# Selective-scan and attention network on one core: the first delta on VectorE, operations with a lower bound on their place, and a new set of places

## Chip, cores and metric

The kernel runs on one core of one Trainium2 chip. The metric is the device time of one execution in microseconds, from three timed executions. The same program was also run once under the hardware profiler; that execution's own time and its span (first to last instruction) stand beside the three below.

A core has TensorE (PE, with its weight loads PEld), VectorE (DVE), ScalarE (ACT), GpSimd (POOL) and SyncE (SP). Each engine takes its instructions in the order of the program. In this kernel all DMA transfers are issued from SP, in the order of its queue.

## The reference, cut to what matters

Eight images of 384 channels and 32 x 32 positions pass two layers. The first is a selective scan in both directions with a gated local convolution; the second is causal attention with six heads and a feed-forward network.

```python
def mamba(x, ...):                      # once forwards, once on the reversed sequence; L = 1024
    u, z = split(x @ in_proj_w.T)
    u = silu(causal_conv4(u) + conv1d_b)
    dt, Bm, Cm = split(u @ x_proj_w.T)                    # 24, 16, 16 columns
    delta = softplus(dt @ dt_proj_w.T + dt_proj_b)
    h = exp(delta * A) * h + (delta * u) * Bm             # over the 1024 positions, 16 states
    y = (sum over states of h * Cm + u * D) * silu(z)
    return y @ out_proj_w.T

x1 = x + res_scale * (scale_mod * (fwd + bwd) + sigmoid(conv3x3(xn) + dw_b) * xn)
t = x1 + attention(layernorm(x1))
out = t + (gelu(layernorm(t) @ w_fc.T) @ w_proj.T)        # w_fc and w_proj are Kronecker products
```

## The kernel before

The kernel does not issue its instructions as it goes. Each piece of work is an `op(engine, cost, fn, reads, writes, at=...)`, which is only recorded; `Plan.run` (line 170) then orders all of them and the instructions are emitted in that order. What the plan decides is therefore the order on each engine's queue and the assignment of buffers, nothing else: on the chip no instruction waits for a time, only for its data, its buffers and the instructions in front of it.

`Plan.run` is a list scheduler. It keeps a time for each engine, and at each step takes the operation that can start first. Among operations of an engine that can start within 0.05 us of each other, the one with the smallest `at` (its place, in us) goes first. So a place is a rank: an operation with a late place is taken early if its engine has nothing else to do. A few rules modify this. ACT prefers the table that it has loaded by `STAY` us of rank (line 110). A DMA that was not given a place by hand waits until the modelled backlog of transfers is under 50 us. Buffers of a kind are handed out by place: 26 general tiles `t`, 12 `dA`, 3 PSUM banks `b`, 1 PSUM bank `y`, 4 PSUM banks `psm`.

Most places come from `Window` (line 446): the operations recorded inside one share the stretch from `t0` to `t1` in proportion to their costs. DMAs get their place earlier by `MOVE`, and ACT or DVE operations that touch a `psm` bank earlier by `EVICT`. The constants of lines 436 to 443 are these windows. Those in capital letters with a 0 or 1 at the end are in us; the others are in units of `PERIOD`, counted from `HEAD` plus the image's number times `PERIOD` (line 1397).

The work of one image:

- `project(b)` loads the image (`xt`) and half of the input weights (`win`), forms the norm (`sq` on ACT, `pss` on PE), writes `xp`, multiplies (`pi` on PE) and writes the rows to DRAM (`urd`).
- `gates(b)` multiplies with the other half of the weights and writes `uzd` and `xpd` to DRAM.
- `prepare(b)` reads shifted rows (`ct`), convolves them (`pc` on PE), applies SiLU (`u`) and forms `xd` (`px` on PE).
- `deltas(b)` calls `delta(b, d, c, ...)` for three blocks of 128 channels and two directions. `delta` computes softplus on ACT (line 891) and six elementwise operations of 128x1024 on POOL (lines 898, 899, 900, 902 and twice 913). Their results, `de` and the three bf16 parts of `du`, go to DRAM (`ded`, `dusd`).
- `scans(b)` runs 96 groups. Each loads `dA` from `ded` and, for every four, `du` from `dusd`; ACT takes the exponential (line 994), PE spreads `du` over the states (the `b` matmul of line 1009), DVE multiplies and scans two halves (lines 1005 and 1013), POOL multiplies by C (line 1016), and PE sums (`y`).
- `local`, `finish`, `layernorm`, `attention`, `mix`, `forward` do the rest for the image while later images are scanned.

The places of a scan group are given by hand from its step's time: loads at `-LOAD`, exponentials at `-DECAY`, POOL products at `-PRODUCTS`, sums at `-SUMS`; with a negative constant the place is later.

Before the first scan stand `setup_early`, `project(0)`, `prepare(0)`, the first `deltas(0)`, and `setup_zeros` (line 572), which writes zeros to the last quarter of each `dusd`. Set up for later use are `setup_late` (line 583: residual scales, local convolution weights `tapw`/`wlm`, `D2`) and `setup_layer1` (line 612: the attention weights copied to `wqkv` in DRAM, `bvc`, `w_fc1`, `w_p1`, `kr2`). The first reader of `bvc` is line 1282 of the attention.

Of the kernel before, what the change touches and what calls it, by code (L numbers as in the profile page):

```python
# [19 lines left out]
L = H * W  # L20
# [45 lines left out]
class Val:  # L66


    __slots__ = ("kind", "shape", "dtype", "name", "t", "slot", "writes", "reads", "left", "end", "first")
# [4 lines left out]


class Op:
    __slots__ = ("engine", "cost", "fn", "vals", "allocs", "at", "waits", "users", "ready", "table", "done", "nbytes", "index", "after", "placed", "urgent")


def act(n):  # L80
# [7 lines left out]
def pool(n):  # L88
    return 0.1 + n * 0.0022
# [15 lines left out]
class Plan:  # L105
# [1 line left out]
    DRAIN = 0.19  # L107
    SLACK = 0.1
    SWITCH = 1.3
    STAY = 50.0  # L110
    BACKLOG = 50.0
    LANDING = 1.0
    DMA_LATENCY, DMA_RATE = 2.5, 262e3
# [5 lines left out]
    def op(self, engine, cost, fn, reads=(), writes=(), at=None, table=None, nbytes=0, holds=()):  # L119


        o = Op()
        o.engine, o.cost, o.fn, o.table, o.nbytes = engine, cost, fn, table, nbytes
        o.at = self.at if at is None else at
        o.placed = o.urgent = at is not None
        o.vals, o.allocs, o.users, o.ready, o.done = [], [], [], 0.0, None
        deps = set()

# [3 lines left out]
        for v in reads:  # L132
            v, part = v if isinstance(v, tuple) else (v, None)
# [3 lines left out]
        for v in writes:  # L137
            v, part = v if isinstance(v, tuple) else (v, None)
# [31 lines left out]
    def run(self):  # L170
# [3 lines left out]
        ready = {e: [] for e in engines}  # L174
        dma = 0.0
        table = None
# [26 lines left out]
                release(owner[id(v)], t)  # L203

        for o in self.ops:
            if o.waits == 0:
                ready[o.engine].append(o)
        for kind in queue:
# [17 lines left out]
        while len(order) < total:  # L226
# [27 lines left out]
            start, e, o = best  # L254
# [33 lines left out]
def conv_attn_hybrid_kernel(  # L288
# [41 lines left out]
    def mm(out_, lhsT, rhs, first=True, last=True):  # L330
        return nc.tensor.matmul(out_, lhsT=lhsT, rhs=rhs, start=first, stop=last)  # L331
# [101 lines left out]

    EVICT, MOVE, SUMS, PRODUCTS, DECAY, LOAD, PARTS = 111.21, 8.82, 26.97, -2.67, -328.02, -584.01, -478.49

    PROJECT, GATES, CONV, DELTA = (-1.521, -1.371), (-1.067, -1.026), (-0.976, -0.866), (-0.889, -0.365)
    LOCAL, OUTPUT, NORM, ATTEND = (0.661, 0.853), (1.005, 1.032), (1.082, 1.173), (1.202, 1.761)
    MIX, FORWARD = (1.787, 1.854), (1.855, 2.07)  # L440

    PROJECT0, EARLY, CONV0, DELTA0 = (-400.622, -296.945), (-523.036, 67.185), (-160.273, 70.933), (131.8, 263.184)
    GATES0, ZEROS, LATE, PROJECT1, GATES1 = (177.592, 252.86), (56.018, 117.713), (263.977, 276.95), (-19.453, 206.415), (352.446, 448.404)
    CONV1, DELTA1, LAYER1 = (250.186, 263.964), (271.922, 425.403), (675.476, 1110.704)

    class Window:


        def __init__(self, t0, t1, start=0.0):
            self.t0, self.t1 = start + t0, start + t1  # L450

        def __enter__(self):
            self.first = len(plan.ops)
# [1 line left out]
        def __exit__(self, *_):  # L455
            ops = [o for o in plan.ops[self.first :] if not o.placed]
            total, done = sum(o.cost for o in ops), 0.0
            for o in ops:
                early = MOVE if o.engine == "SP" else 0.0
                if o.engine in ("DVE", "ACT") and any(v.kind == "psm" for v in o.vals):  # L460
                    early = EVICT
                o.at = self.t0 + (self.t1 - self.t0) * done / total - early
                done += o.cost
                o.placed = True


    def array(shape, name, dtype=F32):
# [400 lines left out]
    def delta(b, d, c, du, xd):  # L868
# [26 lines left out]
            nc.scalar.activation(w.t, w.t, AF.Identity, bias=minus)  # L895

        op("ACT", 4 * act(L) + 0.2, logs, [], [e, ln, w], table=EXP)
        op("POOL", pool(L), lambda: nc.gpsimd.tensor_sub(w.t, e.t, w.t), [e], [w])
        op("POOL", pool(L), lambda: nc.gpsimd.tensor_add(de.t, de.t, ln.t), [ln], [de])
        op("POOL", pool(L), lambda: nc.gpsimd.tensor_add(de.t, de.t, w.t), [w], [de])  # L900
        dma(lambda: ded[d][s].t[chans(c)], lambda: de.t, [de], [(ded[d][s], c)], P * L * 4)
        op("POOL", pool(L), lambda: nc.gpsimd.tensor_mul(du.t, de.t, du.t), [de], [du])
        for k in range(3):
            part = Val("t2", [P, L], f"part_{n}_{k}", BF16)
            op("ACT", act(L), lambda part=part: nc.scalar.copy(part.t, du.t), [du], [part])  # L905
            for hf in range(NH):
                dma(
                    lambda k=k, hf=hf: dusd[d][s].t[c * RG : (c + 1) * RG, hf, k],
                    lambda part=part, hf=hf: part.t[:, half(hf)], [part], [(dusd[d][s], (c, k, hf))], P * HALF * 2,
                )  # L910
            if k < 2:
                op(
                    "POOL", pool(L), lambda part=part: nc.gpsimd.tensor_sub(du.t, du.t, part.t), [part], [du]  # L913
                )

    def scans(b, t0, period):
# [63 lines left out]
    def group(b, a, d, j, r, at, du3, bc):  # L980
# [18 lines left out]
        halves = [(hf, Val("b", [P, HALF], f"b_{n}_{hf}")) for hf in (range(NH - 1, -1, -1) if d else range(NH))]  # L999
        for hf, v in halves:  # L1000
            rr = slice((r * NH + hf) * KI, (r * NH + hf + 1) * KI)
            op("PE", 0.24, lambda v=v, rr=rr: mm(v.t, dup[rr, :], du3.t[rr, j]), [du3], [v], at=-1000.0 + at * 1e-3)
        for i, (hf, v) in enumerate(halves):
            op(
                "DVE", dve(HALF), lambda v=v, hf=hf: nc.vector.tensor_mul(v.t, v.t, bc.t[:, 0, half(hf)]), [(bc, 0)], [v],  # L1005
# [388 lines left out]

    PERIOD, HEAD = 393.0, 65.75

    def stretch(span, b):
        return Window(span[0] * PERIOD, span[1] * PERIOD, HEAD + b * PERIOD)  # L1400
# [8 lines left out]
        deltas(0, *made)  # L1409
    with Window(*GATES0):  # L1410
        gates(0)
    with Window(*ZEROS):
        setup_zeros()
    with Window(*LATE):
        setup_late()
    with Window(*PROJECT1):
        project(1)
    with Window(*GATES1):
        gates(1)
    with Window(*LAYER1):  # L1420
        setup_layer1()
    for b in range(B):
        scans(b, HEAD + b * PERIOD, PERIOD)
# [96 lines left out]
```

## Time and profile before

| | us |
|---|---|
| three timed executions | 4003.02 (median), 3989.68, 4006.04 |
| the profiled execution | 4019.04 |
| its span | 4017.1 |
| first scan instruction starts | 153.2 |
| last scan instructions (L1013) end about | 3747 |
| ACT table loads (L1456), 226 of 1283 ns | 290.0 |
| dA loads, 768 of 512 KB; wait of ACT L994 for them | 234.0 |

The profile's groups are named by line, engine, operation and tile. The helper `dma` gives all transfers line 414 and the helper `mm` most matmuls line 331, so these are told apart by their tiles. "Idle before" is the time that an engine waited ahead of an instruction, with what ended the wait. The start of a transfer in the order of time is the start of its issue on SP, not its landing.

### The profile page before, as it was taken

The page shows a single profiled execution, that of the slowest core. Times are in us where ns is not written, and L with a number is a line of the kernel's source. Part 1 is how long each engine was busy: PE and PEld are TensorE (multiplying, and loading weights), DVE is VectorE, ACT ScalarE, POOL GpSimd, SP SyncE. Part 2 cuts the span into 40 slices and gives each one's busy share as a digit, 9 for nine tenths or more (in the row PEclk, how much of TensorE's full clock was granted, in tenths as well). Part 3 has the DMA queues.
Part 4 walks back from the last instruction along what each step waited for, and adds up shares of the span by engine and source line. Part 5 has one row for each costly group of instructions (what it writes and reads, how often), then busy time and mean ns, then how long its engine had stood idle before and what let it go on. Part 6 is the DMA issues. An engine that isn't in the chain of part 4 may idle for free.

```text
span 4017.1 us, 54053 instructions
## 1 busy us (share of the span) xinstructions
PE 3709.8 (92%) x17970; PEld 1404.8 (35%) x17970; DVE 3332.5 (83%) x4403; ACT 2825.4 (70%) x4468; POOL 2997.6 (75%) x2370
## 2 busy tenths in 40 slices
PE   7577879899999999999999999999999999999998
PEld 2111112443234432444224432444324432443363
DVE  1498979978988989889988999889998899999522
ACT  4756647776788857888678867888678867676364
POOL 1988877997579965899569975899669975776231
PEclk9677678899998999999999999989999999999998
DMA  7989997679976898769976799669986698578100
GB/s 249 270 243 262 255 258 218 178 225 239 270 213 179 236 238 259 205 187 251 269 232 199 226 253 285 190 185 255 260 242 194 181 255 240 147 192 218 49 20 25
DMA packets 301998, 858.92 MB, mean 214 GB/s; under 512 B 38312, under 2 KB 91576, under 8 KB 301720
## 3 DMA queue, kind: packets, MB, share of 16 engines
q1 hardware_dynamic: 301720, 855.47, 76.4%
q8 instruction: 143, 2.34, 0.3%
q14 instruction: 135, 1.11, 0.1%
HBM read 696.44 MB, written 160.68 MB: 213 GB/s over the span
## 4 chain that ended last, share of the span: by engine, by line
PE 53%; DVE 14%; DMA 10%; POOL 8%; issue 4%; ACT 2%; SPq 0%; POOLq 0%; DVEq 0%; ACTq 0%
DVE dA L1013 7%; PE b L331 7%; PE pc L331 6%; PE y L331 5%; PE pi L331 4%; DMA dA<-ded 4%; POOL dA L1016 4%; DVE b L1005 3%; PE t L1250 3%; PE s L331 3%; PE pk L331 3%; PE pvv L331 3%; PE pq L331 2%; DVE mx L1186 2%; POOL p L1240 2%
## 5 line engine op out<-in xcount | busy, mean ns | idle before, releaser
L1016 POOL TENSOR_TENSOR dA<-dA,bc 128x1024 f32<-128x1024 f32 x768 | 1806.1, 2363 | 605.0 <-DVE dA L1013 506.4
L1013 DVE TENSOR_TENSOR_SCAN dA<-dA,b 128x512 f32<-128x512 f32 x1536 | 1854.3, 1234 | 92.7 <-ACT dA L994 90.3
L1005 DVE TENSOR_TENSOR b<-b,bc 128x512 f32<-128x512 f32 x1536 | 996.9, 681 | 173.2 <-PE b L331 161.4
L994 ACT ACTIVATE dA<-dA,nA 128x1024 f32<-128x1024 f32 x768 | 863.4, 1145 | 272.3 <-DMA dA<-ded 234.0
L331 PE MATMUL b<-du,dup 32*128 32x512 bf16 x1536 | 609.4, 408 | 181.0 <-DVE dA L1013 158.8
L331 PE MATMUL y<-dA,sel 128*32 128x512 f32 x3072 | 489.2, 663 | 11.2 <-POOL dA L1016 8.3
L331 PEld LDWEIGHTS <-dup 32*128 32x128 bf16 x1536 | 132.9, 92 | 935.4 <-issue 903.0
L1186 DVE TENSOR_REDUCE mx<-s 128x1 f32<-128x512 f32 (+3 forms) x576 | 288.7, 547 | 186.1 <-PE s L331 182.3
L1240 POOL TENSOR_SCALAR p<-p,den 128x512 f32<-128x512 f32 (+3 forms) x576 | 327.1, 586 | 86.0 <-DVE den L1232 79.3
L1193 ACT ACTIVATE p<-s,mx 128x512 f32<-128x512 f32 (+3 forms) x576 | 329.4, 578 | 75.0 <-DVE mx L1186 74.1
L1257 ACT COPY pT<-t 128x512 f32<-128x512 f32 (+2 forms) x480 | 245.9, 546 | 129.2 <-PE t L1250 123.1
L331 PE MATMUL pi<-xp,win 128*128 128x512 f32 x576 | 312.4, 650 | 10.4 <-DVE xp L696 4.5
L1250 PE MATMUL t<-ident,p 128*128 128x128 f32 x1728 | 281.6, 298 | 29.7 <-POOL p L1240 14.0
L1456 ACT ACT_TABLE_LOAD x226 | 290.0, 1283 | 4.0
L331 PE MATMUL s<-k,q 64*128 64x512 f32 (+3 forms) x1152 | 283.7, 544 | 9.2 <-ACT p L1193 8.6
L1250 PEld LDWEIGHTS t<-ident,p 128*128 128x128 f32 x1728 | 200.1, 149 | 164.8 <-issue 74.0
L331 PE MATMUL pc<-pT,v 128*64 128x128 f32 x3456 | 251.0, 289 | 5.3 <-ACT pT L1257 4.9
L331 PEld LDWEIGHTS pc<-pT,v 128*64 128x64 f32 x3456 | 193.9, 142 | 100.5 <-ACT pT L1257 31.2
L913 POOL TENSOR_TENSOR u<-u,part 128x1024 f32<-128x1024 f32 x96 | 204.9, 2134 | 10.5 <-ACT part L905 9.9
L905 ACT CAST part<-u 128x1024 bf16<-128x1024 f32 x144 | 150.5, 1045 | 64.8 <-DMA dusd<-part 49.9
L1365 ACT ACTIVATE g<-ph 128x512 f32<-128x512 f32 x192 | 104.1, 595 | 118.4 <-PE ph L331 117.4
L331 PEld LDWEIGHTS y<-dA,sel 128*32 128x32 f32 x3072 | 75.4, 112 | 286.2 <-issue 152.6
(184 smaller groups left out, 4776.1 us busy)
## 6 DMA issues: line engine op xcount, KB each, us to landing
dA<-ded SPq DMA_DIRECT2D x768, 512.0 KB
ct<-urd SPq DMA_DIRECT2D x96, 513.5 KB
du<-dusd SPq DMA_DIRECT2D x96, 512.0 KB
xs<-xpd SPq DMA_DIRECT2D x96, 432.8 KB
dusd<-part SPq DMA_DIRECT2D x288, 128.0 KB
ded<-de SPq DMA_DIRECT2D x48, 512.0 KB
uz<-uzd SPq DMA_DIRECT2D x48, 512.0 KB
bc<-bcd SPq DMA_DIRECT2D x32, 512.0 KB
```

Of the source, the lines that this page charges most:

```text
L331: return nc.tensor.matmul(out_, lhsT=lhsT, rhs=rhs, start=first, stop=last)
L913: "POOL", pool(L), lambda part=part: nc.gpsimd.tensor_sub(du.t, du.t, part.t), [part], [du]
L994: "ACT", act(L) + 0.1, lambda: nc.scalar.activation(dA.t, dA.t, AF.Exp, scale=nA.t[:, g : g + 1]),
L1005: "DVE", dve(HALF), lambda v=v, hf=hf: nc.vector.tensor_mul(v.t, v.t, bc.t[:, 0, half(hf)]), [(bc, 0)], [v],
L1013: nc.vector.tensor_tensor_scan(t, t, v.t[:, rev], h, ALU.mult, ALU.add)
L1016: op("POOL", pool(L), lambda: nc.gpsimd.tensor_mul(dA.t, dA.t, bc.t[:, 1]), [(bc, 1)], [dA], at=at - PRODUCTS)
L1186: lambda sc=sc, g=g, w=k1 - k0, hh=hh: nc.vector.tensor_reduce(mx.t[:, g, hh : hh + 1], sc[hh].t[:, 0:w], AX.X, ALU.max, negate=True), [sc ...
L1193: nc.scalar.activation(ps[g].t[:, hh, 0 : k1 - k0], sc[hh].t[:, 0 : k1 - k0], AF.Exp, bias=mx.t[:, g, hh : hh + 1], accum_out=den.t[:, g, ...
L1240: nc.gpsimd.tensor_scalar(t, t, den.t[:, g, hh : hh + 1], 1.0, ALU.mult, ALU.mult)
L1250: nc.tensor.transpose(t.t[:, o + j * P : o + (j + 1) * P], ps[g].t[:, hh, j * P : (j + 1) * P], ident)
L1257: nc.scalar.copy(pT[g].t[:, hs[0] : hs[-1] + 1, 0:w], t.t[:, 0 : len(hs) * w].rearrange("p (h w) -> p h w", w=w))
L1456: nc.scalar.preload_act_table_set(table)
```

## The change

Four things are changed together.

1. The six elementwise operations of `delta` go to DVE, with a cost of 1.2 in the plan, for the first image's first block in the first direction. All other deltas keep POOL.
2. A window can be `held`: its operations are not ready in the plan before their place. `ZEROS`, `LATE`, `PROJECT1` and `LAYER1` are held.
3. All constants of places are new, with `PERIOD`, `HEAD`, and `STAY` 25 in place of 50.
4. The plan's cost of a `b` matmul is 0.325 in place of 0.24.

No instruction besides these six changes engine, and no data is computed in another way.

```diff
-    __slots__ = ("engine", ..., "placed", "urgent")
+    __slots__ = ("engine", ..., "placed", "urgent", "held")
...
-    STAY = 50.0
+    STAY = 25.0
...
         o.placed = o.urgent = at is not None
+        o.held = False
...
         for o in self.ops:
+            if o.held:
+                o.ready = o.at
             if o.waits == 0:
                 ready[o.engine].append(o)
...
-    EVICT, MOVE, SUMS, PRODUCTS, DECAY, LOAD, PARTS = 111.21, 8.82, 26.97, -2.67, -328.02, -584.01, -478.49
+    EVICT, MOVE, SUMS, PRODUCTS, DECAY, LOAD, PARTS = 82.85, 10.31, 27.98, -31.81, -95.38, -1000.42, -591.88

-    PROJECT, GATES, CONV, DELTA = (-1.521, -1.371), (-1.067, -1.026), (-0.976, -0.866), (-0.889, -0.365)
-    LOCAL, OUTPUT, NORM, ATTEND = (0.661, 0.853), (1.005, 1.032), (1.082, 1.173), (1.202, 1.761)
-    MIX, FORWARD = (1.787, 1.854), (1.855, 2.07)
+    PROJECT, GATES, CONV, DELTA = (-1.524, -1.369), (-1.117, -1.031), (-0.978, -0.848), (-0.925, -0.363)
+    LOCAL, OUTPUT, NORM, ATTEND = (0.668, 0.848), (1.0, 1.02), (1.149, 1.17), (1.202, 1.761)
+    MIX, FORWARD = (1.784, 1.828), (1.855, 2.047)

-    PROJECT0, EARLY, CONV0, DELTA0 = (-400.622, -296.945), (-523.036, 67.185), (-160.273, 70.933), (131.8, 263.184)
-    GATES0, ZEROS, LATE, PROJECT1, GATES1 = (177.592, 252.86), (56.018, 117.713), (263.977, 276.95), (-19.453, 206.415), (352.446, 448.404)
-    CONV1, DELTA1, LAYER1 = (250.186, 263.964), (271.922, 425.403), (675.476, 1110.704)
+    PROJECT0, EARLY, CONV0, DELTA0 = (-245.3, -129.175), (-714.373, 90.417), (-128.151, 81.389), (29.762, 164.363)
+    GATES0, ZEROS, LATE, PROJECT1, GATES1 = (225.887, 251.93), (29.21, 60.597), (208.002, 221.031), (-257.494, 100.613), (376.438, 377.438)
+    CONV1, DELTA1, LAYER1 = (127.612, 279.646), (321.852, 516.462), (580.149, 926.317)
...
-                o.placed = True
+                o.placed, o.held = True, self.held
...
-        op("POOL", pool(L), lambda: nc.gpsimd.tensor_sub(w.t, e.t, w.t), [e], [w])
-        op("POOL", pool(L), lambda: nc.gpsimd.tensor_add(de.t, de.t, ln.t), [ln], [de])
-        op("POOL", pool(L), lambda: nc.gpsimd.tensor_add(de.t, de.t, w.t), [w], [de])
+        first = b == 0 and d == 0 and c == 0
+        name, cost, engine = ("DVE", 1.2, nc.vector) if first else ("POOL", pool(L), nc.gpsimd)
+        op(name, cost, lambda: engine.tensor_sub(w.t, e.t, w.t), [e], [w])
+        op(name, cost, lambda: engine.tensor_add(de.t, de.t, ln.t), [ln], [de])
+        op(name, cost, lambda: engine.tensor_add(de.t, de.t, w.t), [w], [de])
         dma(lambda: ded[d][s].t[chans(c)], lambda: de.t, [de], [(ded[d][s], c)], P * L * 4)
-        op("POOL", pool(L), lambda: nc.gpsimd.tensor_mul(du.t, de.t, du.t), [de], [du])
+        op(name, cost, lambda: engine.tensor_mul(du.t, de.t, du.t), [de], [du])
...
-                    "POOL", pool(L), lambda part=part: nc.gpsimd.tensor_sub(du.t, du.t, part.t), [part], [du]
+                    name, cost, lambda part=part: engine.tensor_sub(du.t, du.t, part.t), [part], [du]
...
-            op("PE", 0.24, lambda v=v, rr=rr: mm(v.t, dup[rr, :], du3.t[rr, j]), [du3], [v], at=-1000.0 + at * 1e-3)
+            op("PE", 0.325, lambda v=v, rr=rr: mm(v.t, dup[rr, :], du3.t[rr, j]), [du3], [v], at=-1000.0 + at * 1e-3)
...
-    PERIOD, HEAD = 393.0, 65.75
+    PERIOD, HEAD = 405.15, 84.77
...
-    with Window(*ZEROS):
+    with Window(*ZEROS, held=True):
         setup_zeros()
-    with Window(*LATE):
+    with Window(*LATE, held=True):
         setup_late()
-    with Window(*PROJECT1):
+    with Window(*PROJECT1, held=True):
         project(1)
...
-    with Window(*LAYER1):
+    with Window(*LAYER1, held=True):
         setup_layer1()
```

## The prediction, made before the changed kernel was run

> **What bounds the kernel now.** I read the page's engine totals first, then its chain of waits, then busy time by stage, then the order of time around the start. All fences are of the kernel before.
>
> ```profile
> PE 3709.8 (92%) x17970; PEld 1404.8 (35%) x17970; DVE 3332.5 (83%) x4403; ACT 2825.4 (70%) x4468; POOL 2997.6 (75%) x2370
> ...
> PE 53%; DVE 14%; DMA 10%; POOL 8%; issue 4%; ACT 2%; SPq 0%; POOLq 0%; DVEq 0%; ACTq 0%
> ```
>
> No engine is full, but TensorE is nearest and has half of the chain. Cut into stages by the scans (first at 153, 192 per image, last at 3747 us), busy time reads:
>
> ```profile
> 0.00:152.00 152.00, 104.24 (x293) 40.47 (x294) 18.37 (x74) 85.84 (x110) 58.41 (x63) 0.89 0.81 247
> 152.00:547.00 395.00, 299.16 (x974) 61.51 (x973) 351.76 (x407) 240.95 (x256) 353.40 (x173) 0.69 0.92 259
> 547.00:995.00 448.00, 401.97 (x2035) 154.87 (x2035) 392.18 (x514) 304.10 (x495) 372.13 (x291) 0.89 0.80 220
> ...
> 1905.00:2360.00 455.00, 440.66 (x2242) 169.95 (x2240) 414.14 (x542) 354.13 (x561) 372.30 (x291) 0.99 0.83 234
> ...
> 3750.00:4017.00 267.00, 248.66 (x1319) 126.48 (x1318) 70.29 (x141) 129.06 (x327) 54.84 (x146) 0.96 0.09 33
> ```
>
> After the stretch come PE, PEld, DVE, ACT, POOL busy, the granted clock, the DMA share and GB/s. Four regimes: a start of 152 us in which nothing is scanned; the first image, with DMA at 0.92 and VectorE at 351.8 of 395; the steady images, with TensorE at 440.7 of 455, so 14 us idle; and a tail of 267 us on TensorE, with 18 us idle. What shortens the start moves all that follows. In the steady part an order can win back at most TensorE's gaps, unless it also lets the first scans do more.
>
> The start's last links, in the order of time on POOL, SyncE's queue and VectorE:
>
> ```profile
> 102.24 2.35 POOL L898 TENSOR_TENSOR w<-e,w 128x1024 f32<-128x1024 f32 x1 [19.22 <-ACT w L895]
> 104.54 2.37 POOL L899 TENSOR_TENSOR de<-de,ln 128x1024 f32<-128x1024 f32 x1
> 106.98 2.35 POOL L900 TENSOR_TENSOR de<-de,w 128x1024 f32<-128x1024 f32 x1
> 109.41 2.35 POOL L902 TENSOR_TENSOR u<-de,u 128x1024 f32<-128x1024 f32 x1
> 111.72 2.36 POOL L898 TENSOR_TENSOR w<-e,w 128x1024 f32<-128x1024 f32 x1
> 114.03 2.14 POOL L913 TENSOR_TENSOR u<-u,part 128x1024 f32<-128x1024 f32 x1
> 116.11 2.37 POOL L899 TENSOR_TENSOR de<-de,ln 128x1024 f32<-128x1024 f32 x1
> 118.43 2.15 POOL L913 TENSOR_TENSOR u<-u,part 128x1024 f32<-128x1024 f32 x1
> ```
>
> ```profile
> 126.85 2.48 SPq L414 DMA_DIRECT2D dusd<-part  x2
> 129.86 3.95 SPq L414 DMA_DIRECT2D uzd<-us  x2
> 133.90 2.49 SPq L414 DMA_DIRECT2D dusd<-part  x2
> 136.49 1.99 SPq L414 DMA_DIRECT2D ded<-de  x1
> 138.53 2.73 SPq L414 DMA_DIRECT2D dA<-ded  x2
> 141.30 0.58 SPq L414 DMA_DIRECT2D du<-dusd  x1
> ```
>
> ```profile
> 151.99 1.30 DVE L1005 TENSOR_TENSOR b<-b,bc 128x512 f32<-128x512 f32 x2 [77.58 <-PE b L331]
> ```
>
> The six POOL operations of the first delta run from 102.2 to 120.6 us with two of the second delta between them. The third part is cast at 122.5 to 123.6 on ACT, written at 126.9, and the du load that needs it is issued at 141.3, behind writes of the second delta (133.9, 136.5). It lands 10 us later. VectorE had idled for 77.6 us.
>
> **What the Trainium skill says.** "VectorE: DVE Perf Modes", section The TRN2 errata, gives an fp32 tensor_tensor of N elements (N+151)/0.96 ns; my estimate from that page for N=1024 is 1.22 us. The trace has the 128x512 product with a PSUM operand at 681 ns and two of them in 1.30 us, which agrees in size; 128x1024 with both operands in SBUF is not in it. "SBUF — State Buffer", section Who interferes with whom, says that a VectorE instruction with two SBUF inputs contends with a POOL instruction that reads SBUF. No row separates this out. "ScalarE: Activation LUTs", What ACT_TABLE_LOAD costs, gives 1283 ns and a drain; the page's row has 226 loads of 1283 ns, and L1456 shows no such drain as idle time (4.0 us in all). "Perfetto Trace Analysis", Identifying the Most-Contended Engine, warns that matmul busy time is no measure of roofline. So I use TensorE's gaps only as an upper bound on what an order can return.
>
> **Part by part.** The sum is against the profiled execution's 4019.0 us (span 4017.1, 2 us around it). This lies 16 us above the median of 4003.0 and above the highest of the three, so I carry the difference over to the median.
>
> 1. First delta on VectorE. Removed from POOL: 4 x 2.35 + 2 x 2.14 = 13.7 us. Added on VectorE: 6 x 1.2 = 7.2 us, in the 77.6 us in which it idles, so the engine time is free. On the path 6.5 us go from the operations and up to 4.7 from the second delta's two in between. ACT can give some back: its logs of the second delta (105.3 to 109.8) may stand before the first cast. From 102.2, 7.2 of VectorE and three casts of 1.05 put the third part near 113, with hand-overs 114, against 123.6. The du load waits behind the second delta's writes, but POOL reaches these earlier too, free of 13.7 us. I take -9; bounds -12 and -5 (if every VectorE operation waits for a POOL one through the shared port). If VectorE's idleness were gone it would cost 7.2 us of its own queue.
>
> 2. Weights of layer 1 (LAYER1, held). Their 16 DMA issues run at 20.2 to 36.1 us, 12.2 us on SyncE, and move 2.3 MB. Behind them in the queue stands urd<-ut, issued at 36.8 though its first rows were evicted at 30.4; the ct loads, which wait for urd, begin at 44.2. Held, the weights go to places 570 to 800, where the 650:700 slice of the trace has a DMA share of 0.67. In their stead come eight zero writes (ZEROS, place 24 to 47), 10.6 us of issue at 71.9 now. So one block of the queue replaces another, partly later: -4, bounds -9 and +3. The eight POOL selects on kr (4.0 us) go into a stage where POOL has 76 us free. bvc's place is 707 and the first reader of bvc runs at 717.3; if attention comes 16 us earlier, finished contexts hold the four PSUM banks for up to about 10 us. I cost it at 0, bound +10.
>
> 3. The second image's projection (PROJECT1). Its new window opens at -257, ahead of PROJECT0's -245: its three image loads, at -268 to -257, are placed before the first image's at -256 to -252. Three such loads land 1.3 us apart now (sq starts at 13.6, 14.9, 16.2), so the first projection slips by +4. In return its pss matmuls, which stand between the last conv matmuls from 64.3 to 70.9 us, should be over by then: -6.6 if so, since u is finished at 75.4 only after the last conv. I take -4 for this return, bounds -6.6 and 0; the part's net is 0. Holding itself binds only for the last 28% of the window, which is past time 0.
>
> 4. LATE, held at about 200 to 221. The nine tapw loads that block SyncE for 12.3 us at 271 move some 70 us earlier, and the scans go from 14 to 7 in that slice now; the block stays. The two D loads, issued at 18.8 us now, are needed by the first y at 219.5. With 12 dA buffers, about 46 us of scans at 3.83 each, a lateness of some us is absorbed. 0, bounds -5 and +8.
>
> Parts 1 to 4: -9 - 4 + 0 + 0 = -13, bounds -29 and +20.
>
> 5. New places, STAY 25, and the 0.325 for the b matmul. They add and remove no instruction except table loads; they reorder all five queues. Moved most is LOAD, by which dA loads go 416 us later in rank; DECAY lets the dA exps go 233 us earlier; the POOL products go 29 us later. The plan gave a b matmul 0.24 us; its row has 0.408 (0.384 median), so the plan's TensorE was too short by 1536 x 0.144 to 0.168 = 221 to 258 us. The correction takes 131 of it. TensorE idles 99 us in 995 to 3750 (17, 15, 14, 12, 19, 22). Neither end is excluded: all the gaps won is -99, a spoilt order has no floor in the trace and is priced as rival D. I take a fifth, -20: the correction is right in direction and repairs about half of that error, and 14 us per image are few. Fewer STAY means more loads at 1.283 us; ten more per image are 13 us of ACT, against its 101 idle.
>
> 6. The tail. 267 us, of which about 19 are the sixth image's feed-forward left over (14 ph and 20 pz passes, 3.85 per 4+4, and 12 pe passes at 0.43). The forward window ends later relative to the scans, so I take 0, bounds -19 and +10.
>
> Sum: -13 - 20 = -33, that is 3986 for a profiled execution and 3970 for the median.
>
> **Rivals.** B: more is won. The start gives 13, the gaps about half (50), the left-over feed-forward 19: -82, 3921. For it speaks that the plan's b was wrong by more than TensorE's whole idle time; against it, that TensorE is 97% busy already.
>
> C: the gain of the start is taken up again. The first image runs at a DMA share of 0.92 and must move the same bytes sooner, the weights included, and the rest reorders for nothing: 4003. For it: the chain at 544 to 590 us is bc, dusd and dA transfers. Against it: VectorE, not DMA, is busy 89% there.
>
> D, slower: dA loads come late. Ranked 416 us later, each of 768 loads gives way to any ready weight, gather or write. ACT's dA exps wait 234.0 us for these loads now, and VectorE waits 91.9 us in 38 cases for those exps. It decides once a load's landing (up to 18 us in the chain) and what is issued before it eat the 46 us of the twelve buffers. If the 91.9 double and half is hidden by TensorE's own backlog, +46: 4049. Against it: the exps' earlier place.
>
> **Numbers.** Chances: A (forecast, 3945 to 3990 by itself) 0.40, B 0.18, C 0.17, D 0.25. A measurement of this kernel tells about 0.5% from no change, 3983 to 4023. Faster: 0.37 of A, 0.18 of B, 0.02 of C, 0.57. Same: 0.03 + 0.13 + 0.02 = 0.18. Slower: 0.02 + 0.23 = 0.25. The range 3905 to 4060 takes in B and D with their bounds.
>
> **What would show it.** Step 1: six VectorE rows at 1.2 us from about 100 us, and the first b product near 139 rather than 152. Step 2: no wqkv load before 500 us; urd<-ut issued before 36.8. Step 3: xt loads in two threes before the first sq, no pss between the last conv matmuls. Step 5: TensorE's gaps under 99 us in six images, and the b row's wait for dA unchanged. It is wrong if the first product is no earlier, or if a stage grows: dA waits on VectorE past 92 us mean D, many more than 226 table loads an error in STAY.

## The result, and the profile after

| | before | after |
|---|---|---|
| timed executions, us | 4003.02 (3989.68 to 4006.04) | 4039.77 (4026.71 to 4059.63) |
| profiled execution, us | 4019.04 | 4039.78 |
| first scan starts | 153.2 | 158.0 |
| image 0 (its first scan to the next image's) | 407.1 | 388.6 |
| images 1 and 2 | 456.3, 473.6 | 453.7, 468.2 |
| images 3 to 6, mean | 458.9 | 472.8 |
| image 7 | 422.1 | 413.8 |
| from the last scan to the end | 269.3 | 264.4 |

The changed kernel is slower: ratio 1.0092, 95% interval 1.0065 to 1.0119. The forecast was 3970 us and faster. By the start of image 3 the changed kernel is 22 us ahead; images 3 to 6 give back 56 and turn the sign. The lengths of stages are those of the one profiled execution of each kernel. These two differ by 21 us and the medians by 37, since the profiled execution of the kernel before is 16 us above its median.

From the page of the changed kernel, the engine totals, the chain of waits, and the rows of the scan, of its exponentials, of the b matmul and of the table loads:

```profile
PE 3691.7 (91%) x17970; PEld 1409.0 (35%) x17970; DVE 3335.6 (83%) x4409; ACT 2841.1 (70%) x4484; POOL 2989.2 (74%) x2364
...
PE 40%; DVE 23%; DMA 12%; ACT 6%; issue 5%; POOL 4%; SPq 0%; DVEq 0%; POOLq 0%; ACTq 0%
...
L1020 DVE TENSOR_TENSOR_SCAN dA<-dA,b 128x512 f32<-128x512 f32 x1536 | 1856.5, 1234 | 104.0 <-ACT dA L1001 90.6
...
L1001 ACT ACTIVATE dA<-dA,nA 128x1024 f32<-128x1024 f32 x768 | 861.4, 1145 | 273.7 <-DMA dA<-ded 270.3
L334 PE MATMUL b<-du,dup 32*128 32x512 bf16 x1536 | 596.4, 399 | 191.6 <-DVE dA L1020 173.5
...
L1463 ACT ACT_TABLE_LOAD x242 | 310.5, 1283 | 4.2
```

The work is the same. The chain is what ended last, followed back from the end; TensorE's part in it fell from 53% to 40% and VectorE's rose from 14% to 23%. The wait on VectorE for dA, the sign named for rival D, has not grown (90.6 against 91.9 us). Sixteen more table loads are 20.5 us on an engine that is idle 30% of the time.

Where the time went by stage: of the changed kernel, the start, the first image, a stretch of steady images and images 3 to 6; then images 3 to 6 of the kernel before (columns as in the prediction).

```profile
0.00:152.00 152.00, 92.86 (x287) 35.58 (x290) 30.84 (x77) 93.47 (x117) 57.14 (x56) 0.82 0.78 252
152.00:547.00 395.00, 302.26 (x1006) 68.32 (x1003) 355.04 (x412) 228.41 (x243) 334.70 (x164) 0.78 0.93 257
1905.00:2360.00 455.00, 434.95 (x2159) 167.07 (x2159) 393.82 (x518) 347.82 (x551) 360.37 (x285) 0.97 0.80 221
...
1468.00:3359.00 1891.00, 1795.68 (x8957) 694.04 (x8955) 1650.14 (x2165) 1435.93 (x2255) 1492.91 (x1158) 0.97 0.81 224
```

```profile
1490.00:3325.00 1835.00, 1775.60 (x8959) 685.89 (x8958) 1654.45 (x2164) 1416.39 (x2238) 1490.95 (x1158) 0.98 0.82 230
```

In images 3 to 6 VectorE does the same work (1650 and 1654 us) in 56 us more. The stretch of 455 us that held 542 VectorE instructions now holds 518. TensorE shows the same loss from its side: for the same matmuls it is idle 95 us in place of 59 and busy 20 us longer, at a mean clock of 0.97 against 0.98. The view of waits by engine for these four images names what VectorE and TensorE stood at (total, times, longest). Of the changed kernel:

```profile
DVE mx L1193 <- PE s L334: 71.7, 35, 6.7
DVE dA L1020 <- ACT dA L1001: 59.1, 32, 7.3
DVE b L1012 <- PE b L334: 31.6, 38, 4.2
DVE xr L1078 <- PE pm_a L334: 31.0, 8, 4.1
DVE fy L1352 <- ACT pv_f L339: 11.8, 5, 3.8
...
DVE uz L977 <- DMA uz<-uzd: 8.9, 7, 2.7
...
PE b L334 <- DVE dA L1020: 46.2, 72, 2.4
```

And of the kernel before:

```profile
DVE mx L1186 <- PE s L331: 63.2, 55, 8.2
DVE dA L1013 <- ACT dA L994: 55.3, 24, 8.2
...
DVE uz L970 <- DMA uz<-uzd: 1.8, 1, 1.8
...
DVE fy L1345 <- ACT pv_f L336: 0.2, 1, 0.2
...
PE b L331 <- DVE dA L1013: 13.0, 37, 1.2
```

Three waits on VectorE are new or grown: `xr` behind `pm_a`, `fy` behind `pv_f`, and `uz` behind its load. Their growth is 31.0 + 11.6 + 7.1 = 49.7 us, against 56 lost; `mx` adds 8.5, and some smaller ones fall. VectorE's whole idle time grew by 60 us. One hole that returns in every steady image shows how they come together. SyncE's queue and then VectorE, from 2042 us, of the changed kernel:

```profile
2042.71 2.11 SPq L417 DMA_DIRECT2D out<-x  x2
2046.93 0.38 SPq L417 DMA_DIRECT2D uz<-uzd  x1
...
2059.98 3.92 SPq L417 DMA_DIRECT2D dA<-ded  x6
```

```profile
2054.09 0.74 DVE L977 SCALAR_TENSOR_TENSOR uz<-uz,D,y 128x512 f32<-128x512 f32 x1
2058.97 1.89 DVE L1078 SCALAR_TENSOR_TENSOR xr<-pm_a,xr 128x512 f32<-128x512 f32 x3 [4.14 <-PE pm_a L334]
2064.46 1.89 DVE L1078 SCALAR_TENSOR_TENSOR xr<-pm_a,xr 128x512 f32<-128x512 f32 x3 [3.60 <-PE pm_a L334]
2070.13 2.54 DVE L1020 TENSOR_TENSOR_SCAN dA<-dA,b 128x512 f32<-128x512 f32 x2 [3.78 <-ACT dA L1001]
```

The `uz` load of a finished block goes out at 2046.9, so the closing operation (which empties the only y bank) runs 42.8 us after the block's last y sum; in the kernel before it runs 20.7 us after. Until then no sum of the next block can run, no dA buffer comes free, and between 2019.97 and 2059.98 no dA load is issued. VectorE has no scan from 2052.6 to 2070.1. This looks like a cause. Experiment 4 takes the wait away.

### The profile page after: what moved, and what is told of

Read it like the earlier page. It is cut to its first block, busy times and chain, and to the rows that moved or that the text cites. A ratio compares the mean times of both kernels' runs of the same rounds, so it can differ in the third digit from the quotient of the medians.

```text
span 4037.8 us, 54155 instructions
## 1 busy us (share of the span) xinstructions
PE 3691.7 (91%) x17970; PEld 1409.0 (35%) x17970; DVE 3335.6 (83%) x4409; ACT 2841.1 (70%) x4484; POOL 2989.2 (74%) x2364
## 4 chain that ended last, share of the span: by engine, by line
PE 40%; DVE 23%; DMA 12%; ACT 6%; issue 5%; POOL 4%; SPq 0%; DVEq 0%; POOLq 0%; ACTq 0%
DVE dA L1020 12%; DVE b L1012 6%; DMA dA<-ded 5%; PE b L334 5%; PE pc L334 4%; PE y L334 4%; PE s L334 3%; PE t L1257 3%; PE pq L334 3%; PE pk L334 2%; DVE mx L1193 2%; PE pvv L334 2%; DMA xs<-xpd 2%; PE pi L334 2%; POOL dA L1023 2%
## 5 line engine op out<-in xcount | busy, mean ns | idle before, releaser
L1020 DVE TENSOR_TENSOR_SCAN dA<-dA,b 128x512 f32<-128x512 f32 x1536 | 1856.5, 1234 | 104.0 <-ACT dA L1001 90.6
L1001 ACT ACTIVATE dA<-dA,nA 128x1024 f32<-128x1024 f32 x768 | 861.4, 1145 | 273.7 <-DMA dA<-ded 270.3
L334 PE MATMUL b<-du,dup 32*128 32x512 bf16 x1536 | 596.4, 399 | 191.6 <-DVE dA L1020 173.5
L334 PE MATMUL y<-dA,sel 128*32 128x512 f32 x3072 | 473.7, 652 | 19.0 <-DVE uz L977 10.1
L1264 ACT COPY pT<-t 128x512 f32<-128x512 f32 (+1 forms) x480 | 246.5, 547 | 105.6 <-PE t L1257 100.3
L334 PE MATMUL pi<-xp,win 128*128 128x512 f32 x576 | 297.9, 626 | 0.9 <-ACT pT L1264 0.5
L334 PE MATMUL pvv<-wqkv,xr 128*128 128x128 f32 x1152 | 158.0, 284 | 0.0
## 6 DMA issues: line engine op xcount, KB each, us to landing
ct<-urd SPq DMA_DIRECT2D x96, 513.5 KB
```

The costliest lines, as they stand in the source:

```text
L1001: "ACT", act(L) + 0.1, lambda: nc.scalar.activation(dA.t, dA.t, AF.Exp, scale=nA.t[:, g : g + 1]),
L1020: nc.vector.tensor_tensor_scan(t, t, v.t[:, rev], h, ALU.mult, ALU.add)
L1264: nc.scalar.copy(pT[g].t[:, hs[0] : hs[-1] + 1, 0:w], t.t[:, 0 : len(hs) * w].rearrange("p (h w) -> p h w", w=w))
```

## The experiments

Ratios are to the kernel before, run beside each on the same chip. "3 to 6" is the mean length of images 3 to 6; "y" is the wait from the last y sum to the closing operation for the six blocks of image 4 (us). The last three columns are of one profiled execution each. e12, which keeps the order of the kernel before, has 464.6 where that has 458.9, with 4020 against 4019 us in all: a difference of some 6 us per image can't be read.

| run | ratio (95%) | first scan | 3 to 6 | y |
|---|---|---|---|---|
| before, profiled | | 153.2 | 458.9 | 21 13 1 1 34 0 |
| after, profiled | 1.0092 (1.0065 to 1.0119) | 158.0 | 472.8 | 43 16 9 24 39 0 |
| e1_cost_alone | 1.0280 (1.0256 to 1.0304) | 152.2 | 478.0 | 0 13 18 16 46 3 |
| e2_after_old_cost | 1.0146 (1.0104 to 1.0187) | 161.3 | 469.5 | 48 10 0 8 40 0 |
| e3_start_alone | 1.0257 (1.0231 to 1.0283) | 158.5 | 474.1 | 43 6 6 19 45 0 |
| e4_steady_alone | 1.0154 (1.0123 to 1.0185) | 157.5 | 469.3 | 43 16 9 24 46 0 |
| e5_cost_hair | 1.0234 (1.0199 to 1.0268) | 153.0 | 476.3 | 43 6 6 20 40 0 |
| e16_cost_up | 1.0108 (1.0078 to 1.0137) | 152.0 | 469.7 | 23 4 0 11 40 0 |
| e17_head_later | 1.0000 (0.9980 to 1.0021) | 151.5 | 459.7 | 21 13 1 1 34 0 |
| e15_after_hair | 1.0094 (1.0059 to 1.0128) | 158.6 | 469.9 | 28 11 0 20 39 0 |
| e18_start_other_cost | 1.0053 (1.0024 to 1.0083) | 159.0 | 467.6 | 19 13 0 11 40 0 |
| e13_after_own_u | 1.0184 (1.0159 to 1.0208) | 162.0 | 469.8 | 1 2 0 0 2 1 |
| e14_before_own_u | 1.0090 (1.0060 to 1.0120) | 150.1 | 464.8 | 1 0 0 0 0 1 |
| e6_after_b_later | 1.0112 (1.0078 to 1.0145) | 159.7 | 469.1 | 45 17 12 25 48 1 |
| e7_before_b_later | 1.0059 (1.0036 to 1.0083) | 152.1 | 462.6 | 21 13 1 1 33 2 |
| e10_delta_alone | 1.0067 (1.0046 to 1.0088) | 164.7 | 458.4 | 21 13 1 1 39 0 |
| e12_delta_in_place | 1.0011 (0.9992 to 1.0029) | 150.4 | 464.7 | 21 13 1 1 35 0 |

### 1. The change in halves

e1 is the kernel before with only the new cost; e2 the changed kernel with the old one; e3 the changed kernel with cost, scan constants, steady windows, `PERIOD`, `HEAD` and `STAY` of before; e4 the kernel before with exactly these from the change.

```diff
 e1
-            op("PE", 0.24, lambda v=v, rr=rr: mm(v.t, dup[rr, :], ...
+            op("PE", 0.325, lambda v=v, rr=rr: mm(v.t, dup[rr, :], ...
```

> The kernel before with one number changed: the plan's cost of a b matmul is 0.325 in place of 0.24. Theory K (the cost alone makes the slow order: with TensorE too long in the plan, the steady order gets looser): slower than before by 1% or more, 4040 or above, and image lengths near 470 in place of 458. Theory L (the new places make it, the cost is right in direction as the prediction had it): within 0.5% of before or faster, 3985 to 4020. Theory M (any change to a tuned set of places loses its fit, whatever it is): slower by 0.5 to 2%, with no particular wait.

> The kernel after with the b matmul's cost back at 0.24. Theory K: the loss goes, about 4003. Theory L: no change, about 4040. Theory M: as slow as after or slower, 4030 to 4080, since the new places were fitted to 0.325.

> The kernel after with the cost, STAY, PERIOD, HEAD, the scan constants and all windows of the steady images back as before; left of the change are the first delta on VectorE, the held windows, and the windows of the start (PROJECT0 to LAYER1). If the loss is made in the steady order (K or L): the start's share alone, first b product at 152 to 157 and 4000 to 4015. Theory M: 4020 to 4050, because the steady places no longer meet the start that they were fitted to.

> The kernel before with only the steady part of the change: cost, STAY, PERIOD, HEAD, scan constants and the windows of the steady images; no delta on VectorE, no held window, the start's windows as before. K or L: as slow as after, 4030 to 4060, with image lengths near 470. Theory M: slower than after, 4050 or above.

All four are slower than the kernel before. The cost by itself is the worst of them, yet taking it out of the changed kernel doesn't help. Start alone (2.6%) and steady part alone (1.5%) together make 0.9%. Parts that add up to more than the whole, and cost more alone than together, are not parts in the sense of a sum. Theory K (the cost makes it) falls with e2, theory L (the places make it, the cost is right) with e1 and e3. Theory M is left, though e3's 4095 us is above the 4020 to 4050 that it named. `STAY` needs no run: with 25 or 50 the plan makes the same order of either kernel, so the table loads come from the places.

### 2. A hair's breadth

If the parts don't add, what does a change cost that is too small to mean anything?

```diff
 e5, e16: the kernel before; e15: the changed kernel
-            op("PE", 0.24, ...       e5: 0.239     e16: 0.241
-            op("PE", 0.325, ...      e15: 0.324
 e17: the kernel before
-    PERIOD, HEAD = 393.0, 65.75
+    PERIOD, HEAD = 393.0, 66.75
```

> The kernel before, with the plan's cost of a b matmul at 0.239 in place of 0.24, and nothing else. Theory M (the order of the kernel before is one fit among many, and any change of what the plan reckons gives another order, worse by a per cent or so): slower by more than 0.5%, about 4015 to 4040, though the cost is all but the same; the place of the loss is again VectorE's waits in the steady images. Theory K (the larger cost makes a slow order): a cost that is lower by 0.4% changes nothing, ratio 1.00 within 0.5%. Theory L (the places make it): the places are those of the kernel before, so ratio 1.00 within 0.5%.

> The kernel before with the plan's cost of a b matmul at 0.241 in place of 0.24 (0.239 cost 2.3%). Theory M (the order of the kernel before is a rare fit; either neighbour gives another order, and an ordinary one is slower): slower by over 0.5%, 4025 to 4105. If only a lower or a much higher cost is bad (a real optimum at or above 0.24): within 0.5% of before.

> The changed kernel with the plan's cost of a b matmul at 0.324 in place of 0.325. The same change on the kernel before (0.24 to 0.239) cost 2.3%. Theory M in its strong form (the changed kernel is a fit of its own, and each small step off it costs): slower than the changed kernel by 0.5% or more, 4060 to 4100. In its weak form (only the kernel before is a rare fit, the changed one lies among ordinary orders): 4030 to 4055, no difference from the changed kernel. That the places themselves cost (theory L): no difference either, and images 3 to 6 as in the changed kernel, 470 to 475.

> The kernel before with HEAD at 66.75 in place of 65.75: all places of the steady images are 1 us later against those of the start, and among themselves unchanged. The instruction order differs in a small part of the places only. It is the control for theory M: a change of a constant that leaves nearly all of the order as it was costs nothing, within 0.5% of before, with the steady images' waits between last y sum and closing operation as in the kernel before (20.7, 13.1 and 34 us). If it is slower by over 1%, it isn't the extent of the reordering that counts.

A cost that is off by 0.4% makes the kernel before 2.3% slower downwards and 1.1% slower upwards. What it does to the order is large: of the 5049 operations on TensorE's queue, 1937 (e5) and 1915 (e16) must be moved to get back the old order; for the whole change they are 2372, and for e17, which costs nothing, 37. The step from 0.325 to 0.324 moves 1469 of them and changes no time beyond the intervals. So neither of the two reordered neighbours matches the order of the kernel before, and the one neighbour of the changed kernel is as good as that. This fits theory M in its weak form (the kernel before is a rare fit, the changed one an ordinary order). It rests on three neighbours. The strong form, that the changed kernel too is a fit which any step spoils, fell with e15.

### 3. Does a run of the start alone measure the start?

```diff
 e18: as e3, but
-            op("PE", 0.24, ...
+            op("PE", 0.25, ...
```

> The run with the start's parts alone (first delta on VectorE, held windows, start windows new; scan constants, steady windows, PERIOD and HEAD as before) had 1.0257 at a b cost of 0.24. This is the same with 0.25. Theory M: the two differ by more than 0.5% from each other, either way, though the cost stands for nothing; then what a run of a part alone measures is the draw of an order and not the part. Theory L (the start's places themselves cost 2.6%): the same as that run, 1.02 to 1.03.

It doesn't: with the same first delta, held windows and start windows, 2.57% became 0.53%. Two points of it come from which order the plan happened to make.

An order can lose in another way than by waits. Images 3 to 6 of e3, of e18 and of e5:

```profile
1492.00:3388.00 1896.00, 1812.91 (x8960) 701.87 (x8960) 1652.42 (x2164) 1440.65 (x2255) 1493.34 (x1158) 0.95 0.80 223
1488.00:3358.00 1870.00, 1789.56 (x8982) 692.80 (x8980) 1651.79 (x2164) 1441.47 (x2263) 1493.24 (x1158) 0.97 0.82 227
1504.00:3409.00 1905.00, 1815.52 (x8963) 693.41 (x8962) 1654.98 (x2164) 1435.50 (x2250) 1493.23 (x1158) 0.96 0.80 222
```

Of the 26 us between e3 and e18, 23 are TensorE's busy time for the same matmuls, and only 3 its idle time. In e5, 40 of the 70 us lost against the kernel before are busy time. The longer busy time goes with a lower granted clock (0.95 and 0.96, against 0.97 in e18 and 0.98 in the kernel before). It comes with the order: the executions of e3 and e5 have mean clocks of 0.921 to 0.926, those of the kernel before beside them 0.930 to 0.941. By which path the order sets the clock was not tested. In the changed kernel's images 3 to 6 this is the smaller part, 20 of 56 us at most.

Image 0 tends to follow the start's windows: 383.0 to 397.6 us in six kernels with them (after, e2, e3, e6, e15, e18), 397.0 to 407.1 in the ten without, but 409.1 in e13, which has them too.

### 4. The hole at the y bank

The u half of `uz` gets 2 KB of its own, in the changed kernel (e13) and in the one before (e14).

```diff
+        "us": (1, HALF * 4),
...
+            us = Val("us", [P, HALF], f"us_{b}_{a}")
+            dma(lambda us=us: us.t, lambda v=v: v.t[0], [(v, "u")], [us], ..., at=at - 20.0)
+            dma(lambda uz=uz: uz.t[:, 1], lambda v=v: v.t[1], [(v, "z")], [uz], ..., at=at - 20.0)
...
-                    uz.t[:, 0], uz.t[:, 0], D2.t[:, a : a + 1], y.t, ALU.mult, ALU.add
+                    us.t, us.t, D2.t[:, a : a + 1], y.t, ALU.mult, ALU.add
```

> The changed kernel, where the u half of uz has a buffer of 2 KB of its own, so that the closing operation of a y block no longer waits for a general buffer; its load is split in two (48 more transfers). Theory H (the hole: the y bank waits for a late uz, 42.8 us in the first block of every image, all twelve dA buffers stay full, the scans stop): the wait between the last y sum and the closing operation falls under 15 us in all blocks, the gaps over 12 us between dA loads fall from 115 us per image to under 90, images 3 to 6 shorten from 472.8 towards 460, the time falls to 3990 to 4015. Theory M (an order is worth what its fit is worth; the hole is one of several places where a lesser fit shows its loss): the wait at y is gone or shorter, but another takes its place, images stay at 468 or more, time 4035 to 4100.

> The kernel before with the same buffer of its own for the u half of uz. Theory H: its own lags (20.7 and 34 us in two blocks of each image) go too, images of 459 us shorten by 3 to 8, time 3965 to 3990. Theory M: slower than before by over 0.5%, 4020 to 4090, though a wait has been taken away, since the order is a new one.

The wait is gone in both (table) and both are slower, by 0.9% each against their own kernel. The waits of VectorE and TensorE in images 3 to 6 of e13:

```profile
DVE dA L1019 <- ACT dA L1000: 87.5, 28, 10.8
DVE xr L1056 <- PE pg L334: 33.9, 6, 7.9
...
DVE fac L1230 <- POOL fac L1227: 11.4, 10, 5.5
DVE dA L1019 <- POOL w L905: 7.4, 1, 7.4
...
PE b L334 <- DVE dA L1019: 43.7, 72, 1.9
```

Other waits now stand where `uz` stood, among them a wait for dA that has grown from 59.1 to 87.5 us. So taking the hole away brings no gain. That it costs nothing isn't shown: the edit also issues 48 more transfers and lets the plan find a new order, so by experiment 2 only a gain well over a per cent would have shown. The table speaks against it as the cause, too: e1 has no wait in the first block of image 4 and is the slowest run.

### 5. TensorE's wait at the b matmul

46.2 us against 13.0 could be the cause if TensorE stands at a b whose bank isn't free while other work waits behind it. After the plan has made its order, each b goes one TensorE operation back, where that one's inputs allow; all else stays.

```diff
     order = plan.run()
+    order = later_b(order)
```

> The changed kernel with its order kept, but for this: each b matmul of the scans is issued one TensorE operation later, wherever the next operation has all its inputs in front of it. Theory P (TensorE, which takes its queue in order, stands at a b whose bank VectorE has not freed, 46.2 us in images 3 to 6 against 13.0 before; this is where the 13 us per image go): TensorE's waits at b fall by more than half and the time by 20 to 45 us, to about 4000 to 4020. Theory S (the wait is a symptom: VectorE has stopped for lack of dA, because the y bank waits for a late uz): no gain, 4030 to 4050, the 40 us holes between dA loads stay. A third outcome, slower by more than 10 us, would say that VectorE needs b as early as it comes.

> The kernel before with its order kept, but each b matmul of the scans one TensorE operation later, as in the run on the changed kernel. Theory P: TensorE's waits at b (13.0 us in images 3 to 6) fall by half, the time by up to 10 us: ratio 0.995 to 1.00. Theory S: 1.00. If VectorE needs b as early as it comes: slower by more than 0.5%, VectorE's wait for b grows.

In images 3 to 6 of e6, the wait of TensorE at b and that of VectorE for b:

```profile
PE b L363 <- DVE dA L1049: 4.8, 6, 1.6
```

```profile
DVE b L1041 <- PE b L363: 72.5, 85, 3.6
```

TensorE's wait is gone (46.2 to 4.8 us; 13.0 to 2.8 in e7), and there is no gain in either: VectorE's wait for b rose from 31.6 to 72.5 us (from 33.3 to 102.1 in e7). What TensorE no longer waits, VectorE waits. The edit moves the wait and doesn't remove it; a gain from TensorE's side alone, as theory P expected, is not there.

### 6. The first delta by itself

e12 keeps the order of the kernel before on all engines and issues only the six operations on VectorE. e10 also moves them, the casts, their writes and the first du load as far forward as inputs and buffers allow.

```diff
+        engine = nc.vector if b == 0 and d == 0 and c == 0 else nc.gpsimd
-        op("POOL", pool(L), lambda: nc.gpsimd.tensor_sub(w.t, e.t, w.t), [e], [w])
+        op("POOL", pool(L), lambda: engine.tensor_sub(w.t, e.t, w.t), [e], [w])
...
     order = plan.run()
+    order = early(order, quick)          (e10 only)
```

> The kernel before with its order kept, but for the first delta: its six elementwise operations run on VectorE, and these, the three casts, the writes of de and of the parts and the first du load are issued as early as their inputs and buffers allow. This is step 1 of the prediction without new places. Theory G (the step was right, and the changed kernel lost it to its own order: the logs of other deltas and six dA exps in front of the third cast): third cast done by about 113, the first b product 8 to 13 us earlier than 152, near 141, and the time 5 to 13 us shorter, ratio 0.997 to 0.999. Theory H (another input of the first products, dA or bc, is then late): third cast near 113, first product still later than 148, no gain. Theory I (the first image takes the start's gain up again, rival C): first product near 141, first image longer by the same, ratio 1.00.

> The kernel before, with its order on every engine kept, and only the six elementwise operations of the first delta issued on VectorE from where they stood on GpSimd. It is step 1 by itself: in the run that also moved the casts forward, the third cast waited 7.93 us for the first part's write, because there are two buffers for parts. Theory J (the casts, not the six operations, hold the third part: two part buffers and ACT's queue): VectorE's rows take 1.22 us, but the third cast ends at 120 to 123 in place of 123.6, the du load at 136 to 141, the first b product 0 to 4 us earlier than 152, time within 0.2% of before. Theory G (the prediction's step 1): third cast done by 114 to 116, first product 139 to 144, time 8 us shorter.

The casts on ACT in e10, in the order of time:

```profile
104.69 1.05 ACT L924 CAST part<-u 128x1024 bf16<-128x1024 f32 x1 [3.92 <-DVE u L921]
107.03 1.05 ACT L924 CAST part<-u 128x1024 bf16<-128x1024 f32 x1 [1.29 <-DVE u L932]
116.01 1.05 ACT L924 CAST part<-u 128x1024 bf16<-128x1024 f32 x1 [7.93 <-DMA dusd<-part]
```

Parts have two buffers (`t2`), so the third cast waits until the first part has landed in DRAM, here 10.3 us after its cast ended. ACT takes its queue in order, so the other deltas' `e`, `de` and logs waited behind it. TensorE's queue, in the order of time:

```profile
155.95 3.23 PE L346 MATMUL pd<-xd,w_dt 24*128 24x512 f32 x4 [6.18 <-ACT de L903]
159.11 3.78 PE L346 MATMUL pi<-xp,win 128*128 128x512 f32 x4
162.82 0.61 PE L346 MATMUL b<-du,dup 32*128 32x512 bf16 x3
```

The first b stands behind a `pd` that waited for ACT, and then runs without a wait of its own, 41 us after its du load was issued (121.86). The first product came at 163.5: late, as in theory H, but held by TensorE's queue and not by dA or bc. In e12 the third cast and the first product on VectorE:

```profile
119.06 1.05 ACT L924 CAST part<-u 128x1024 bf16<-128x1024 f32 x1
```

```profile
149.24 1.30 DVE L1028 TENSOR_TENSOR b<-b,bc 128x512 f32<-128x512 f32 x2 [33.28 <-PE b L346]
```

The cast is 3.4 us earlier than before (122.50), the product 2.8. Theory J holds; step 1 without new places is worth about 3 us in the start and nothing measurable in all.

## Why the prediction was wrong, by its steps

**Step 1, the first delta: -9 predicted; the first product came 4.8 us later.** The six instructions were sized right where VectorE was alone. Of the changed kernel, VectorE and then ACT around the three casts:

```profile
99.34 1.23 DVE L909 TENSOR_TENSOR u<-de,u 128x1024 f32<-128x1024 f32 x1
108.39 2.64 DVE L920 TENSOR_TENSOR u<-u,part 128x1024 f32<-128x1024 f32 x1 [7.82 <-ACT part L912]
113.73 2.89 DVE L920 TENSOR_TENSOR u<-u,part 128x1024 f32<-128x1024 f32 x1 [2.71 <-ACT part L912]
```

```profile
107.27 1.09 ACT L912 CAST part<-u 128x1024 bf16<-128x1024 f32 x1
...
112.67 1.03 ACT L912 CAST part<-u 128x1024 bf16<-128x1024 f32 x1
...
118.02 6.33 ACT L1001 ACTIVATE dA<-dA,nA 128x1024 f32<-128x1024 f32 x6
124.25 1.03 ACT L912 CAST part<-u 128x1024 bf16<-128x1024 f32 x1
```

The logs ended at 95.5 (102.2 before), and VectorE had du at 100.6, 11 us ahead of the kernel before. From there ACT's queue took it all: other deltas' `e` and `de` stand in front of the first cast (107.27), their logs in front of the second and third, and six dA exponentials, which the new `DECAY` lets go early, in front of the third. It ends at 125.3, against 123.6. The step that failed is "three casts of 1.05 put the third part near 113": it priced the casts and not what stands in front of them. That ACT could give back some by its logs was said, for the first cast only. The du load was then issued at 141.79 (141.30) and its b ran at 156.4, 14.6 us later in place of about 10, with `ct` loads of the second image around it (21 against 14 issued before the first scan).

**Step 2, LAYER1 held: -4 predicted, not found.** No `wqkv` load from the inputs is issued before image 1, as said, but `urd<-ut` goes out at 37.36, not before 36.8: three `xpd` writes and `wcd` now stand in front.

**Step 3, projection of the second image: 0 predicted, about right.** Five of the six image loads come first and the first `sq` slips by 0.8 us, not 4; the `pss` are gone from between the conv matmuls as said, but twelve `pi` matmuls took that place, and `u` is done at 74.3 against 75.4.

**Step 4, LATE: 0.** Nothing here contradicts it.

**Not in the sum: image 0, -18.5.** This image runs at a DMA share of 0.93, and 9 `ct` loads are issued in it instead of 18. Nine of 513.5 KB at 257 GB/s are 18 us, an estimate that would cover it. The transfers moved into the start and image 1 (rival C looked at this stage and expected the opposite). Some 5 of the 18.5 only make up for the later start. Image 0 tends to follow the start's windows (experiment 3); the count of loads alone was not tried.

**Step 5, new places and the cost: -20 predicted; images 3 to 6 lost 56 us, images 2 to 7 together 42.** This is the step that failed. Its argument was that the cost's "correction is right in direction". It is wrong twice. First, the true cost was mis-sized: the profile's b row has 0.384 to 0.408, but on TensorE's queue of the changed kernel the next matmul starts 0.31 us after a b:

```profile
2044.44 0.39 PE L334 MATMUL b<-du,dup 32*128 32x512 bf16 x1
2044.75 1.12 PE L334 MATMUL pe<-fz,kr 128*128 128x512 f32 x2
```

So the old value was short by some 0.07, not 0.15, and the new one is near the truth (0.31 itself was not run). Secondly, and decisively, a more truthful cost is not a better order: alone it cost 2.8%, and in the changed kernel its removal gained nothing. TensorE's idle time from image 2 to 7 rose from 99 us to 131, where a fall was predicted. The fall was taken as a fifth of the idle time, on a direction and no measurement; the sentence that "a spoilt order has no floor in the trace" was the one to build on. `STAY`, for which ten more table loads per image were feared, does nothing at all.

**Step 6, the tail: 0 predicted, -4.9 measured.** Within its bounds.

**Rival D** had the sign and a time 9 us off, by another mechanism: its sign, VectorE's wait for dA, stayed at 90.6 us. ACT's wait for dA loads did rise, from 234.0 to 270.3 us, but it didn't reach VectorE as a longer wait for dA. That the time came out near is luck.

**What is open.** Shown: the loss lies in the steady images; it is of the size that a reordering of the kernel before costs anyway (e5 2.3%, e16 1.1% for a cost off by 0.4%); taking away the wait at the y bank, or TensorE's at b, brings no gain. Which property of the old order is worth its one to two per cent was not found. The waits have a part in it, in e3 and e5 the granted clock has another. No run beat the kernel before; e12, the only piece of the change without cost, can't be told from it.

## What to carry to other kernels

Where a planner orders everything, ask first how far a change of its inputs reorders the queues, and run two or three changes that stand for nothing: their scatter (here 0 to 2.3%) is the size that a real change must exceed, and a part's effect can't be read from one run. Compare busy time and granted clock beside the waits, since an order can lose by either. To price a step in such a kernel, hold the order and change the step alone; for an instruction moved to a faster engine, read what stands in front of its consumer on the consumer's queue and how many buffers lie between. A wait that is seen to empty the pipeline in every image may still be only the place where a loss shows: take it away before you believe it.

## What the runs showed of the hardware

VectorE's fp32 operation on two SBUF inputs of 128x1024 (`tensor_tensor`) takes 1.22 us alone, as estimated from the Trainium skill, "VectorE: DVE Perf Modes", The TRN2 errata. Beside GpSimd's operations it took 2.13 to 2.18 us (e12) and 2.64 to 2.89 us (changed kernel), while GpSimd's own went from 2.35 to 3.2 to 3.4 us. In e10, with no GpSimd operation starting between 95 and 124 us, the same two took 1.23. The Trainium skill, "SBUF — State Buffer", Who interferes with whom, states that a VectorE instruction with two SBUF inputs contends with a GpSimd instruction that reads SBUF, and these runs agree. The size, about double for VectorE, was not expected, and step 1 held it only as a bound. It cost little here, since ACT was later.

TensorE's b matmul has a mean of 399 ns in its row, but where the next matmul follows at once it starts 0.31 us after the b. For a price in a plan the distance of starts counts, not the row.
